# A decoder layer on one core: heads summed on VectorE, layernorm's step on ScalarE, and a re-costed plan

## Chip, cores and metric

The program runs on one core of one Trainium2 chip. The metric is device time in microseconds (us), lower is better. Engines are called by their short names in the profile: PE (TensorE, matrix products), DVE (VectorE), ACT (ScalarE), POOL (GpSimd) and SP (SyncE, which issues the DMAs).

## What is computed

32 sequences of 128 positions with 128 features go through three residual blocks, each followed by a layernorm without gain. All of it is in float32. Cut to its core, for `x` of shape (32, 128, 128):

```python
x = layernorm(x + self_attention(x, W))            # 16 heads of 8 features, no mask
x = layernorm(x + cross_attention(x, ctx, Wq, ...)) # 16 heads, window of 64 positions
x = layernorm(x + ffn(x))                          # two layers, see below

def self_attention(x, W):        # y: x cut into 16 heads of 8
    attn = softmax(y @ y.T / sqrt(8))              # per head, 128 x 128
    o = attn @ x                                   # per head, 128 x 128: the whole x
    return concat_heads(o) @ W                     # W: 16*128 x 128

def layer(x):                    # twice
    q, k, v = shift_token(x) @ wqkv                # 8 heads of 64
    q, k = rotary_xpos(l2norm(q) * qs, l2norm(k) * ks)   # cosines, sines of the swapped halves
    x = x + local_attention(q, k, v) @ wo          # window of 64, softmax
    h = layernorm(shift_token(x)) * lg + lb
    a, g = split(h @ w1 + b1)
    return x + (a * gelu(g)) @ w2 + b2
```

## The kernel before

Everything stays on the chip between the blocks. The 32 sequences are cut into ten groups of 2, 3, 3, 4, 4, 4, 4, 4, 3 and 1 (`SIZES`). There are four stages: self-attention, cross-attention and the two layers. A group passes through the stages one after another, and several groups are in flight at once, each in another stage.

**Order.** No operation is issued where it stands in the code. Each call `op(engine, ns, fn, reads, writes, ...)` records one step with a booked duration in ns. `Plan.issue` (line 132) then simulates the five engines: it keeps a clock per engine, a delay `hop` between engines, a price for a new activation table, a price for a change of TensorE's tile shape, and the free buffers of each ring. Each time it issues the step that can start first. What comes out is a fixed order for each engine's queue, in which the chip then runs, each instruction waiting for its inputs by semaphores. The order in which steps are offered is set by constants at the top: `LAGS` says how far a stage trails the one before it, in units of four sequences; `SPREAD`, `CLOSE` and `EARLY` stretch these places; `AHEAD` bounds how far a step may be drawn forward; among the steps that start within `NEAR` ns, the one recorded first is taken. Steps with `port=True` are those of VectorE and GpSimd that the plan keeps from running beside each other.

**Buffers.** `m` is a ring of eight PSUM banks of 128x512 float32. `big` (128x1032), `mid` (128x520), `xb`, `xc`, `sm` and others are rings in SBUF; `RINGS` and `KEEP` are their sizes and how many are kept back for older steps.

**Self-attention** (`self_half`, line 571) handles one sequence and eight heads: a half. The product with W is moved in front: `zs = x W_h` for each head (TensorE, L579; copied out by ScalarE, L586), with a column of ones behind each head. The scores (L542) are reduced to their maxima (VectorE, L421), GpSimd splits these in two bfloat16 parts (L435, L436), TensorE turns and subtracts them (L442, L452), ScalarE takes exp (L600). Then TensorE multiplies by `zs` in groups of three, three and two heads (L608): the ones' column yields the row sums. VectorE inverts the sums (L617) and multiplies (L618), writing the normalized heads back into `zs`. GpSimd adds the eight heads in a tree, four, two and one wide (L628), and adds the result to the residual tile `x0` (L632).

**Layernorm** (`layernorm`, line 377) runs five times for each group: VectorE takes the statistics (L382, L389), GpSimd makes the factor and the offset with a power (L397 to L400), and VectorE applies both, one 128x128 instruction for each sequence (L407). `feed_forward` then turns the result on TensorE (L373).

**A layer** (`local_batch`, line 790) projects one sequence to q, k and v with three products of 512 columns (L796) that ScalarE copies out (L801). ScalarE squares q and k (L807), VectorE sums the squares (L810), GpSimd raises the sums to -1/2 (L813, L814). GpSimd multiplies the swapped halves by the sines (L824), VectorE multiplies q and k by the cosines (L833), adds both (L837) and scales (L840). TensorE turns q and k (L851, copied by ScalarE at L857), makes the masked scores (L865, L871), VectorE takes maxima (L421), ScalarE the exps with their sums (L466), VectorE divides (L885, L886), TensorE turns (L481, copied out at L488), multiplies by v (L900, L907) and projects (L912, L919). The feed-forward part is L944 to L971. Cross-attention uses the same helpers; its own products are at L649, L663, L689 and L724, its normalization at L750 and L751, and its residual sum at L696.

Of the kernel before, what the change touches and what calls it, by code (L numbers as in the profile page):

```python
# [16 lines left out]
P = 128  # L17
# [11 lines left out]
AHEAD = 430  # L29
LAGS = (0, 1.35, 2.75, 4.1)  # L30
RINGS = (23, 16, 6, 4)
KEEP = (2, 3, 5)
NEAR = 0
EARLY = (0, 0.2)
CLOSE = (0.9, 0.85, 0.9, 1, 1, 1, 1.2, 1.05, 0.85, 0.95)
SPREAD = (1.4, 1.0, 0.7, 1.5)
# [40 lines left out]
class Plan:  # L77

# [51 lines left out]
    def issue(self, ahead, near=80.0, hop=60.0, table_ns=1300.0, tiling_ns=160.0, dma_ns=1800.0):  # L132
# [13 lines left out]
        def time_of(k):  # L146
            e = ops[k][0]
            return max([0.0] + [end[d] + (hop if ops[d][0] != e else 0.0) for d in ops[k][3]])
# [5 lines left out]
        shared = 0.0  # L154
# [5 lines left out]
        while len(order) < n:  # L160
            best = None
            for e in engines:
                choice, least = [], None
                for k, t in ready[e]:
                    if k > first + ahead:
                        continue
                    start = max(clock[e], t, shared if ops[k][7] else 0.0)
# [5 lines left out]
                    for vs in need.values():  # L173
                        q = vs[0].ring
                        if len(q.free) < len(vs) + (0 if q.queue[q.head] in vs else q.keep):
                            ok = False
                            break
                        start = max(start, sorted(q.free)[len(vs) - 1][0] + hop)
# [4 lines left out]
                    if e == "PE" and ops[k][8][0] != state:  # L183
                        start += tiling_ns
# [22 lines left out]
            else:  # L207
                end[k] = clock[e] = s + ns
            if tab:
                table[e] = tab  # L210
            if port:
                shared = end[k]
# [19 lines left out]
def decoder_kernel(ctx: ExitStack, tc: tile.TileContext, a: dict, out: bass.AP):  # L232
# [129 lines left out]
    def turned(src, n):  # L362

        tp, t = Val(mring), Val(mid)
        op("PE", 113 * n, turn(src, tp, n), [src], [tp], hold=[t])
        op("ACT", 140 + 113 * n,
# [10 lines left out]
    def layernorm(src, dst, n):  # L377
# [6 lines left out]
        op("DVE", n * 290, stats, [src], [st])  # L384
# [6 lines left out]
        op("DVE", n * 175, aggr, [st], [mv])  # L391
# [10 lines left out]
        op("POOL", 1100 + 260 * n, rest, [], [mv])  # L402

        def apply():
            x, y = group(src.t), group(dst.t)
            for j in range(n):
                nc.vector.tensor_scalar(  # L407
                    y[:, j, :], x[:, j, :], mv.t[:, 8 + j : 9 + j], mv.t[:, 12 + j : 13 + j],
                    ALU.mult, ALU.add,
                )  # L410

        op("DVE", 200 * n, apply, [mv] + ([src] if src is not dst else []), [dst])
# [4 lines left out]
    def maxima(s, nm):  # L417
        for b in range(2):
            op(
                "DVE", 690,  # L420
# [5 lines left out]
    def minus_max(s):  # L426
# [6 lines left out]
        def parts():  # L433
# [4 lines left out]
        op("POOL", 440, parts, [nm], [hl])  # L438
        mp = Val(mring, lambda t: t[:, 0:64].bitcast(BF16))
        op(  # L440
            "PE", 110,
# [4 lines left out]
        op("ACT", 260, lambda: nc.scalar.copy(mT.t, mp.t), [mp], [mT])  # L446
# [10 lines left out]
    def exps_of(s, sums=None):  # L457
# [4 lines left out]
        for b in range(2):  # L462
# [8 lines left out]
            op("ACT", 4 * (345 if sums else 255) + 60, exps, [s[b], (nm, b)],  # L471
# [3 lines left out]
    def turned_half(e, et, b, eng, src):  # L475
# [9 lines left out]
        op("PE", 4 * 113, pe, [src], [tp], hold=[et])  # L485
        copy = nc.vector.tensor_copy if eng == "DVE" else nc.scalar.copy
        op(eng, 690 if eng == "DVE" else 590,
# [6 lines left out]
    def in_slots(src, n, keep_src, moving):  # L494
# [4 lines left out]
        op("ACT", 140 + 113 * n,  # L499
           lambda: nc.scalar.copy(pv.t[:, 0, every], src.t[:, every]), [src], [(pv, 0)])  # L500
        op("POOL", 316 * n,
# [3 lines left out]
        op("ACT", 140 + 113 * n,  # L505
           lambda: nc.scalar.copy(pv.t[:, 1, every], rest.t[:, every]), [rest], [(pv, 1)])
        op("POOL", 316 * n,
# [26 lines left out]
    def scores_of(s, stationary, moving, hh, window=False):  # L534
# [12 lines left out]
        op("PE", 8 * 62 + 432 * window, pe,  # L547
# [22 lines left out]
    def self_half(j, hh, x0, xT, ys):  # L570
# [3 lines left out]
        for b in range(2):  # L574
# [3 lines left out]
                "PE", 875,  # L578
# [6 lines left out]
                "ACT", 590,  # L585
# [10 lines left out]
        op("PE", 8 * 60, lambda: emit_max(s, mT), [mT, (w_self, 2)], s)  # L596
        e = Val(big, heads)
        for b in range(2):
            op("ACT", 590,
# [3 lines left out]
        for k, (h0, n) in enumerate(((0, 3), (3, 3), (6, 2))):  # L603
# [9 lines left out]
            op("PE", 230 * n, pe, [e] + [(zs, i) for i in range(3)], [oz])  # L613
            rl = Val(small)

            def scale(oz=oz, rl=rl, h0=h0, n=n):
                nc.vector.reciprocal(rl.t[:, 0:n], oz.t[:, 0:n, D])  # L617
                nc.vector.tensor_tensor(  # L618
                    zs.t[:, h0 : h0 + n, 0:D], oz.t[:, 0:n, 0:D],
                    rl.t[:, 0:n].unsqueeze(2).to_broadcast([P, n, D]), ALU.mult,  # L620
                )

            op("DVE", 175 + 30 + 133 * n, scale, [oz], [rl, (zs, ("o", k))])

        z = lambda h0, n: zs.t[:, h0 : h0 + n, 0:D]
        for n, ns in ((4, 1270), (2, 730), (1, 450)):
            op("POOL", ns,
               lambda n=n: nc.gpsimd.tensor_tensor(z(0, n), z(0, n), z(n, n), ALU.add),  # L628
               [], [zs], port=n > 1)
# [493 lines left out]
```

## Time and profile before

| | us |
|---|---|
| median of three runs | 1292.23 |
| lowest and highest | 1289.26, 1293.61 |
| the profiled execution | 1292.12 |
| its span, first to last instruction | 1290.3 |
| mean granted clock of TensorE | 0.987 of full |

The profile's first part gives busy time, share of the span and number of instructions of each engine; PEld are TensorE's weight loads, which overlap its products. Records of TensorE overlap too, because products are pipelined, so groups of it sum to more than the engine's busy time. The chain is the work that ended last, followed back from the end: at each step to what released it. A group has the form "line engine operation out<-in"; `m` stands for any of the eight PSUM banks. For one line, median and extremes of the durations are to be had as well: the power of L813 takes 2895 at least, 2910 in the median and 3996 ns at most.

### The profile page before, as it was taken

What the parts mean: (1) busy time and instruction counts of PE and PEld (TensorE: products, weight loads), DVE (VectorE), ACT (ScalarE), POOL (GpSimd) and SP (SyncE); (2) the same over time, 40 slices, a digit from 0 to 9 for tenths busy, and PEclk for the clock granted to TensorE, in tenths of its full rate; (3) what the DMA queues carried; (4) which work ended last, traced back from release to release, by engine and by line L of the source; (5) the groups of instructions that cost most, each with busy time, mean ns of one, the idle gap of its engine ahead of it and who ended that gap; (6) DMA issues with size and microseconds to landing.
All of it is one profiled execution on the core that took longest, in us unless ns stands there. A gap on an engine that the chain in (4) does not pass through costs nothing.

```text
span 1290.3 us, 27579 instructions
## 1 busy us (share of the span) xinstructions
PE 1213.9 (94%) x9730; PEld 888.0 (69%) x9730; DVE 1070.3 (83%) x2134; ACT 966.2 (75%) x2762; POOL 835.3 (65%) x1094
## 2 busy tenths in 40 slices
PE   7988999999979999999999999999999989999996
PEld 4766677776767865777777667778667657567664
DVE  2677889878968888887798889979899999988786
ACT  4564777777867778777778778858889968879863
POOL 2866657765857389555687468653966963786454
PEclk9999999999989999999999999999999989999999
DMA  9886414240154420732005401330300000000000
GB/s 254 209 213 193 124 39 105 56 128 9 37 136 109 99 56 1 174 89 65 20 25 138 124 1 34 94 95 18 97 2 12 18 18 2 9 1 2 2 1 25
DMA packets 173930, 91.44 MB, mean 71 GB/s; under 512 B 155872, under 2 KB 161888, under 8 KB 173536
## 3 DMA queue, kind: packets, MB, share of 16 engines
q1 hardware_dynamic: 173792, 89.67, 27.5%
q8 instruction: 77, 1.26, 0.4%
q14 instruction: 61, 0.50, 0.1%
HBM read 49.79 MB, written 39.85 MB: 69 GB/s over the span
## 4 chain that ended last, share of the span: by engine, by line
PE 45%; POOL 15%; DVE 14%; ACT 6%; issue 3%; DMA 1%; SPq 0%; POOLq 0%; DVEq 0%; ACTq 0%
PE m L796 6%; POOL sm L813 6%; PE m L481 5%; PE m L944 4%; PE m L608 4%; ACT big L466 3%; PE m L900 3%; PE m L579 3%; PE m L871 3%; PE m L912 3%; POOL big L824 3%; PE m L964 3%; PE m L724 2%; DVE sm L421 2%; PE m L542 2%
## 5 line engine op out<-in xcount | busy, mean ns | idle before, releaser
L466 ACT ACTIVATE big<-m,sm 128x128 f32<-128x128 f32 x1024 | 323.0, 399 | 54.5 <-DVE sm L421 53.9
L421 DVE TENSOR_REDUCE sm<-m 128x4 f32<-128x512 f32 x384 | 245.6, 681 | 45.4 <-PE m L871 21.5
L813 POOL TENSOR_TENSOR sm<-sm,nhalf 128x16 f32<-128x16 f32 x64 | 200.8, 3137 | 36.8 <-DVE sm L810 26.7
L628 POOL TENSOR_TENSOR big<-big 128x512 f32<-128x512 f32 (+2 forms) x192 | 163.2, 850 | 83.8 <-DVE big L618 36.8
L824 POOL TENSOR_TENSOR big<-big,layer_w 128x512 f32<-128x512 f32 x128 | 162.4, 1269 | 76.4 <-ACT big L801 71.1
L796 PE MATMUL m<-layer_w,mid 128*128 128x512 f32 x384 | 193.2, 612 | 4.2 <-DVE xb L971 2.1
L481 PE MATMUL m<-ident,big 128*128 128x128 f32 x1024 | 144.4, 276 | 15.4 <-DVE big L886 9.6
L481 PEld LDWEIGHTS m<-ident,big 128*128 128x128 f32 x1024 | 115.7, 141 | 54.9 <-issue 21.9
L579 PE MATMUL m<-self_w,mid 128*128 128x512 f32 x256 | 131.1, 626 | 7.0 <-DMA self_w<-in_self_w 5.7
L608 PEld LDWEIGHTS m<-big,big 128*128 128x128 f32 x1024 | 123.0, 191 | 13.7 <-issue 7.5
L608 PE MATMUL m<-big,big 128*128 128x129 f32 x1024 | 129.9, 276 | 0.9 <-DVE big L618 0.3
L466 ACT ACTIVATION_READ_ACCUMULATOR big<-m,sm 128x1 f32 x512 | 115.9, 226 | 0.0
L586 ACT COPY big<-m 128x512 f32<-128x512 f32 x128 | 75.1, 600 | 38.8 <-PE m L579 38.0
L618 DVE TENSOR_TENSOR big<-m,sm 128x384 f32<-128x384 f32 (+1 forms) x192 | 98.6, 514 | 6.6
L886 DVE TENSOR_TENSOR big<-big,sm 128x512 f32<-128x512 f32 x128 | 98.2, 767 | 4.6 <-DMA slots<-big 0.2
L542 PEld LDWEIGHTS <-big 72*128 72x128 bf16 x1024 | 72.3, 98 | 41.3 <-issue 20.2
L542 PE MATMUL m<-big,big 72*128 72x128 bf16 x1024 | 87.8, 220 | 9.6 <-DMA big<-slots 8.9
L488 ACT COPY big<-m 128x512 f32<-128x512 f32 x128 | 75.0, 598 | 28.3 <-PE m L481 19.4
L796 PEld LDWEIGHTS m<-layer_w,mid 128*128 128x128 f32 x384 | 64.7, 193 | 42.6 <-issue 27.9
L857 ACT COPY big<-m 128x512 f32<-128x512 f32 x128 | 71.6, 608 | 29.7 <-PE m L851 29.1
L944 PE MATMUL m<-mid,layer_w 128*128 128x512 f32 (+7 forms) x240 | 89.5, 516 | 2.7 <-DVE mid L935 1.5
L488 DVE COPY big<-m 128x512 f32<-128x512 f32 x128 | 82.0, 681 | 11.5 <-PE m L481 10.7
(116 smaller groups left out, 2611.4 us busy)
## 6 DMA issues: line engine op xcount, KB each, us to landing
slots<-big SPq DMA_DIRECT2D x384, 96.0 KB
big<-slots SPq DMA_DIRECT2D x128, 288.0 KB
layer_w<-in_layer_w SPq DMA_DIRECT2D x2, 1877.0 KB
mid<-in_xt SPq DMA_DIRECT2D x5, 256.0 KB
mid<-in_xg SPq DMA_DIRECT2D x5, 256.0 KB
mid<-in_ct SPq DMA_DIRECT2D x5, 256.0 KB
out<-xb SPq DMA_DIRECT2D x5, 256.0 KB
self_w<-in_self_w SPq DMA_DIRECT2D x2, 512.0 KB
```

The lines of the kernel that those rows point to most:

```text
L421: lambda b=b: nc.vector.tensor_reduce(nm.t[:, 4 * b : 4 * b + 4], s[b].t, AX.X, ALU.max, negate=True),
L466: nc.scalar.activation(e.t[:, h, :], s[b].t[:, h - 4 * b, :], AF.Exp, bias=nm.t[:, h : h + 1], accum_out=sums.t[:, h : h + 1] if sums else ...
L481: nc.tensor.transpose(tp.t[:, 128 * c : 128 * c + 128], e.t[:, 4 * b + c, :], ident)
L488: lambda: copy(et.t[:, 4 * b : 4 * b + 4, :], tp.t.rearrange("p (c k) -> p c k", c=4)),
L542: nc.tensor.matmul(s[b].t[:, i, :], st[:, h, :], mv[:, h, :], start=not window and i == 0, stop=i == 3,)
L579: lambda zp=zp, h0=h0: nc.tensor.matmul(zp.t, group(xT.t)[:, j, :], attn_w[:, h0 : h0 + 4, :], start=True, stop=True),
L608: nc.tensor.matmul(oz.t[:, i, :], e.t[:, h0 + i, :], zs.t[:, h0 + i, :], start=True, stop=True,)
L628: lambda n=n: nc.gpsimd.tensor_tensor(z(0, n), z(0, n), z(n, n), ALU.add),
L796: lambda hp=hp, i=i: nc.tensor.matmul(hp.t, group(hT.t)[:, j, :], wqkv[l][:, INNER * i : INNER * (i + 1)], start=True, stop=True),
L813: nc.gpsimd.tensor_tensor(rn.t[:, 0:16], rn.t[:, 0:16], nhalf, ALU.pow)
L824: nc.gpsimd.tensor_tensor(r2.t[:, :, :, d0 : d0 + 32], q[:, :, :, d1 : d1 + 32], tabs[l][:, :, d0 : d0 + 32].unsqueeze(2).to_broadcast([P, ...
L944: lambda t=t, off=off, c0=c0, m=m: nc.tensor.matmul(t.t[:m, every], w1[l][:, off + c0 : off + c0 + m], hT.t[:, every], start=True, stop=True),
```

## The change

1. **Self-attention.** VectorE still inverts the row sums. Then, for each head, one instruction multiplies the head in PSUM by its inverse sum and adds it to the residual tile `x0`, eight for a half. The normalized heads are no longer written to `zs`, and GpSimd's four adds for a half are gone.
2. **Cosines.** The product of q and k with the cosines is made for each of the two projections straight from the PSUM bank, into the tile `qr`, beside ScalarE's copy. It replaces the one product of twice the width that read the copy. `qr` is now taken when the projection is issued.
3. **Layernorm.** The factor and the offset are applied by ScalarE, with one per-partition operand for each, in place of VectorE.
4. **Plan.** All booked durations are new. The delay between engines is now a `TAIL` of the engine that ends and a `HOP` of the one that starts; a follower on the same engine may start at the end of the booking. GpSimd and VectorE's `port` steps now exclude each other by a lock for each side. A change of tile shape is booked at 95 or 150 ns. `AHEAD`, `RINGS`, `KEEP`, `NEAR`, `EARLY`, `CLOSE` and `SPREAD` have new values.

```diff
-AHEAD = 430
+AHEAD = 330
-RINGS = (23, 16, 6, 4)
-KEEP = (2, 3, 5)
-NEAR = 0
-EARLY = (0, 0.2)
+RINGS = (23, 17, 6, 4)
+KEEP = (3, 4, 7)
+NEAR = 60
+EARLY = (0.1, 0.2)
-SPREAD = (1.4, 1.0, 0.7, 1.5)
+SPREAD = (1.3, 1.0, 0.7, 1.5)
...
+    TAIL = {"PE": 165.0, "DVE": 82.0, "ACT": 115.0, "POOL": -75.0, "SP": 0.0}
+    HOP = {"PE": 55.0, "DVE": 32.0, "ACT": 36.0, "POOL": 77.0, "SP": 25.0}
...
-            return max([0.0] + [end[d] + (hop if ops[d][0] != e else 0.0) for d in ops[k][3]])
+            return max([0.0] + [
+                end[d] + (self.HOP[e] if ops[d][0] != e else -self.TAIL[e]) for d in ops[k][3]
+            ])
...
-                    start = max(clock[e], t, shared if ops[k][7] else 0.0)
+                    start = max(clock[e], t)
+                    if e == "POOL" or ops[k][7]:
+                        start = max(start, lock["DVE" if e == "POOL" else "POOL"])
...
-                        start += tiling_ns
+                        start += 95.0 if state == "whole" else 150.0
...
         def apply():
             x, y = group(src.t), group(dst.t)
             for j in range(n):
-                nc.vector.tensor_scalar(
-                    y[:, j, :], x[:, j, :], mv.t[:, 8 + j : 9 + j], mv.t[:, 12 + j : 13 + j],
-                    ALU.mult, ALU.add,
+                nc.scalar.activation(
+                    y[:, j, :], x[:, j, :], AF.Identity,
+                    scale=mv.t[:, 8 + j : 9 + j], bias=mv.t[:, 12 + j : 13 + j],
                 )
-        op("DVE", 200 * n, apply, [mv] + ([src] if src is not dst else []), [dst])
+        op("ACT", 365 * n, apply, [mv] + ([src] if src is not dst else []), [dst])
...
             op(
-                "DVE", 690,
+                "DVE", 598,
                 lambda b=b: nc.vector.tensor_reduce(
...
-            def scale(oz=oz, rl=rl, h0=h0, n=n):
+            def scale(oz=oz, rl=rl, n=n):
+                y = group(x0.t)[:, j, :]
                 nc.vector.reciprocal(rl.t[:, 0:n], oz.t[:, 0:n, D])
-                nc.vector.tensor_tensor(
-                    zs.t[:, h0 : h0 + n, 0:D], oz.t[:, 0:n, 0:D],
-                    rl.t[:, 0:n].unsqueeze(2).to_broadcast([P, n, D]), ALU.mult,
-                )
-            op("DVE", 175 + 30 + 133 * n, scale, [oz], [rl, (zs, ("o", k))])
-        z = lambda h0, n: zs.t[:, h0 : h0 + n, 0:D]
-        for n, ns in ((4, 1270), (2, 730), (1, 450)):
-            op("POOL", ns,
-               lambda n=n: nc.gpsimd.tensor_tensor(z(0, n), z(0, n), z(n, n), ALU.add),
-               [], [zs], port=n > 1)
-        y = lambda: group(x0.t)[:, j, :]
-        op("POOL", 450,
-           lambda: nc.gpsimd.tensor_tensor(y(), y(), z(0, 1)[:, 0, :], ALU.add),
-           [zs], [(x0, j)])
+                for i in range(n):
+                    nc.vector.scalar_tensor_tensor(
+                        y, oz.t[:, i, 0:D], rl.t[:, i : i + 1], y, ALU.mult, ALU.add
+                    )
+            op("DVE", 100 + 205 * n, scale, [oz], [rl, (x0, j)])
...
-               [hT, w_layer[l]], [hp], hold=[qk if i < 2 else vs])
-            op("ACT", 590,
+               [hT, w_layer[l]], [hp], hold=[qk, qr] if i < 2 else [vs])
+            op("ACT", 478,
...
+            if i < 2:
+                op("DVE", 620,
+                   lambda hp=hp, i=i: nc.vector.tensor_tensor(
+                       qr.t[:, i], hp.t.rearrange("p (h d) -> p h d", d=LD),
+                       tabc[l][:, i].unsqueeze(1).to_broadcast([P, LH, LD]), ALU.mult),
+                   [hp, w_layer[l]], [(qr, i)])
...
-        op("POOL", 2600, swap, [qk, w_layer[l]], [r2], port=True)
-        qr = Val(big, four)
-        op("DVE", 1240,
-           lambda: nc.vector.tensor_tensor(
-               qr.t, qk.t.rearrange("p (a h) d -> p a h d", a=2),
-               tabc[l].unsqueeze(2).to_broadcast([P, 2, LH, LD]), ALU.mult),
-           [qk, w_layer[l]], [qr], port=True)
-        op("DVE", 1240, lambda: nc.vector.tensor_tensor(qr.t, qr.t, r2.t, ALU.add), [r2], [qr], port=True)
-        op("POOL", 3200, power, [], [rn])
+        op("POOL", 2237, swap, [qk, w_layer[l]], [r2], port=True)
+        op("DVE", 1140, lambda: nc.vector.tensor_tensor(qr.t, qr.t, r2.t, ALU.add), [r2], [qr], port=True)
+        op("POOL", 3171, power, [], [rn])
```

In the changed file the lines that the prediction names stand some lines lower: the adds of point 1 at L631, the product of point 2 at L811, the step of point 3 at L417.

## The prediction

> **What bounds the kernel now.** I read the page's first part, then the chain that ended last, then the stretches of 100 us, then the groups by form, then short pieces of the timeline. The page and its chain:
>
> ```profile
> span 1290.3 us, 27579 instructions
> PE 1213.9 (94%) x9730; PEld 888.0 (69%) x9730; DVE 1070.3 (83%) x2134; ACT 966.2 (75%) x2762; POOL 835.3 (65%) x1094
> ...
> PE 45%; POOL 15%; DVE 14%; ACT 6%; issue 3%; DMA 1%; SPq 0%; POOLq 0%; DVEq 0%; ACTq 0%
> ```
>
> TensorE is covered for 94%, yet the chain runs over it for only 45%: for the other half somebody makes TensorE's next input just in time, most of all GpSimd and VectorE. TensorE's busy time also holds pipeline ends. Its own need, from its tightest rows in the chain: 760 records of 512 columns (L796, L579, L944) at 0.43 us (L796 x4 in 1.72) are 327 us; 1920 of L608, L912, L964 at 0.112 us (L608 x32 in 3.57), 215; 1728 transposes (L481, L851, L373) at 0.109 us (L481 x12 in 1.31), 188; 3072 of L724, L900, L871 at 0.055 to 0.068 us, some 187; the bf16 scores, masks and rest some 235. Together about 1150 us. So 140 us of the span are waits, refills, start and end. Where they lie:
>
> ```profile
> 0.00:100.00 100.00, 86.80 (x623) 61.61 (x623) 58.26 (x145) 55.67 (x131) 57.93 (x134) 1.00 0.86 225
> ...
> 800.00:900.00 100.00, 98.63 (x875) 76.13 (x874) 86.98 (x197) 76.88 (x233) 57.27 (x83) 1.00 0.28 69
> 900.00:1000.00 100.00, 99.37 (x782) 69.61 (x782) 92.12 (x161) 87.42 (x252) 74.63 (x73) 1.00 0.15 38
> 1000.00:1100.00 100.00, 91.37 (x705) 64.93 (x701) 92.87 (x156) 79.58 (x250) 65.72 (x59) 0.97 0.05 12
> ...
> 1200.00:1290.00 90.00, 77.54 (x589) 55.05 (x587) 67.24 (x161) 54.96 (x175) 43.86 (x58) 0.96 0.03 10
> ```
>
> The columns are PE, PEld, DVE, ACT, POOL, granted clock, DMA share, GB/s. Self-attention's normalization ends at 907 us; behind it, with the two layers alone, VectorE is at 92% and TensorE loses time again behind it.
>
> **The groups the change touches**, by form:
>
> ```profile
> L833 DVE TENSOR_TENSOR big<-big,layer_w 128x1024 f32<-128x1024 f32 x64 | 86.0, 1343 | 3.9 <-ACT big L801 3.8
> ...
> L618 DVE TENSOR_TENSOR big<-m,sm 128x384 f32<-128x384 f32 x128 | 71.5, 558 | 4.4
> L407 DVE TENSOR_SCALAR mid<-mid,sm 128x128 f32<-128x128 f32 x64 | 31.4, 546 | 8.2 <-POOL sm L400 8.2
> ...
> L919 DVE TENSOR_TENSOR xb<-m,xb 128x128 f32<-128x128 f32 x32 | 9.1, 288 | 11.8 <-PE m L912 8.0 <-PE m L740 3.1
> ...
> L954 DVE SCALAR_TENSOR_TENSOR mid<-m,cross_w,mid 128x128 f32<-128x128 f32 x4 | 1.3, 336 | 1.0 <-ACT mid L950 1.0
> ```
>
> Each row gives busy us and the mean ns of one; behind the bar the idle time before it and what ended it. The adds exist today as GpSimd's L628, the sum's nearest kin on VectorE as L954 and L919.
>
> The chain is a path of 1290 us, so I price each part by what it has there: I added up the chain's pieces line by line.
>
> **1. Self-attention's adds leave GpSimd.** L628 (163.2 us) and L632 (31.8) go, 195.0 of GpSimd's 835.3 us. On the chain they have 21.9 + 2.8: **-24.7 us**. What is late next is the same sum, now on VectorE:
>
> **2. The sum on VectorE.** Eight fused multiply-adds of 128x128 per half take the place of three products, 512 in all. Each adds into the same x0 tile, and in the built program each waits for the one before. What such a wait costs:
>
> ```profile
> 592.80 0.18 DVE L617 RECIPROCAL sm<-m 128x3 f32<-128x3 f32 x1 [1.08 <-PE m L608]
> 593.01 0.56 DVE L618 TENSOR_TENSOR big<-m,sm 128x384 f32<-128x384 f32 x1
> ...
> 593.90 0.25 DVE L750 RECIPROCAL sm<-m 128x16 f32<-128x16 f32 x1
> 594.18 0.29 DVE L751 TENSOR_TENSOR mid<-m,sm 128x128 f32<-128x128 f32 x1
> ...
> 598.62 0.56 DVE L618 TENSOR_TENSOR big<-m,sm 128x384 f32<-128x384 f32 x1
> 599.09 0.17 DVE L617 RECIPROCAL sm<-m 128x3 f32<-128x3 f32 x1
> ```
>
> A dependent step starts 30 ns after its forerunner ended (593.90 + 0.25 to 594.18); an independent one 85 ns before that end (598.62 + 0.56 to 599.09). With L954's 336 ns a dependent add takes 0.366 us and the last 0.251: three heads 0.21 + 2 x 0.366 + 0.251 = 1.19 us, two heads 0.81, a half 3.19. Before, from the rows, 0.68 + 0.68 + 0.54 = 1.90. So +1.29 x 64 = **+83 us of VectorE**. On the chain L617 and L618 have 13.2 us; times 3.19/1.90: **+9.0 us**. With L919's 288 ns a half is 2.84; with no price on the wait (0.205 an add) 2.25 and the term +2.4; I take L954, the same operation. Queued behind these adds are maxima and PSUM copies that TensorE waits for.
>
> The Trainium skill, "VectorE: DVE Perf Modes", section "The DRAIN you can't avoid", says that chained operations pay the pipeline's flush with or without a semaphore, so the wait is free. The rows above disagree by 0.115 us a step; by the page's rule a step costs the same either way, and this term would be +2.4 us.
>
> **3. Layernorm's step moves to ScalarE.** L407 is 160 instructions in four forms, 72.3 us, 0.452 each. Unhindered four take 1.10 us (1265.66 in the timeline), but:
>
> ```profile
> 1043.13 4.48 POOL L824 TENSOR_TENSOR big<-big,layer_w 128x512 f32<-128x512 f32 x4
> 1043.21 4.48 DVE L407 TENSOR_SCALAR mid<-mid,sm 128x128 f32<-128x128 f32 x4 [1.64 <-POOL sm L400]
> ...
> 1044.45 0.30 PE L373 MATMUL m<-ident,mid 128*128 128x128 f32 x1 [2.11 <-DVE mid L407]
> ```
>
> Each instruction waits out one of GpSimd's, and TensorE's transpose of the tile waits with it. On the chain L407 has 34.2 us, 76 instructions' worth. ScalarE's nearest row is L466 of the same size with one operand per partition: 12 in 3.21 us without the accumulator, 0.27 each; with the accumulator read 0.35. The new form has two such operands; I take 0.31: 76 x 0.31 = 23.6, so **-10.6 us** (-13.7 to -7.6). ScalarE gets 160 x 0.31 = 50 us and stays under 82%; queued behind are its evictions. Table loads in the built order fall from 36 to 34 (2.6 us). If ScalarE is late there, TensorE's turn of the normalized tile is late too.
>
> The Trainium skill, "ScalarE: Activation LUTs", section "What ACT_TABLE_LOAD costs", speaks against this: every per-partition operand adds about 93 ns. With 0.27 + 0.09 = 0.36, an estimate, the term would be -6.8 us; no row here has two such operands.
>
> **4. The cosines' product.** 64 of L833 (86.0 us) become 128 of 512 columns straight from PSUM, nearest L971's form at 685 ns, 0.60 in a run as L488 (four in 2.47): 78 us. On the chain L833 has 10.0 us; the product now stands beside ScalarE's copy, but its successor L837 still needs GpSimd's L824, so I book half, **-5 us** (0 to -10). A bank of PSUM is held until VectorE has read it too.
>
> **5. Port.** L407 and L833 no longer collide with GpSimd. GpSimd's power (L813) takes 2910 ns in the median and 3137 in the mean, 14.5 us in all; 36% lies on the chain. **-2 us**.
>
> **6. GpSimd's queue.** 165 us of GpSimd stay on the chain (L813 72.1, L824 33.5). Load falls by 23%, so these start sooner where they queued behind an add. Bounds 0 and 23% of 165 = 38; starts, not durations, shrink: I take a tenth, **-16 us**.
>
> **7. Order.** Every booking is rewritten, so every queue is re-ordered; TensorE's work is the same 8547 instructions, SyncE's DMA issues the same 560. TensorE changes its tile shape 278 times against 239; sixteen scores took 1.32 against 1.16 us, so 39 x 0.16 = 6 at most: **+3 us**. The rest of the re-planning I book at nothing, between -35 (half the idle and refill time of the middle) and +80: a half's adds are booked at 1.94 us, and by part 2 take 3.19, so 64 x 1.25 = 80 us of VectorE stand in no booking.
>
> Sum: -24.7 + 9.0 - 10.6 - 5 - 2 - 16 + 3 = **-46.3 us**. The profiled execution took 1292.1 us for its span of 1290.3; that gives a span of 1244 and **1246 us**, against the median of 1292.2 alike. VectorE's total hardly changes (+83 - 72 - 8 - some 5 of lock), but it moves from the crowded last 400 us into the first 900.
>
> **Rivals.**
> - *Order pays more.* With the idle time of the first and last 100 us as it is (13 and 12 us) over the need of 1150, and -35 from re-planning: 1211 us. For it: bookings now match rows (L421 598 for 0.60 in a run, L824 2237 for 2 x 1105). Against it: the adds' do not. 14%.
> - *The gain is eaten by banks and buffers.* PSUM has eight banks; held longer for adds and cosines they stall projections. Giving back 30 us: 1276 (1268 to 1296). For it: ScalarE's waits for PE are spread over all evictions, so TensorE runs few banks ahead. 16%, 6 of them within 0.3% of before.
> - *Slower: VectorE becomes the bound in the first 900 us.* If all 80 unbooked us of the adds fall on TensorE, 1246 + 80 = 1326; it ends above 1296 once more than 50 of 80 land. Against it: from 100 to 900 us VectorE is idle 16%, 2 us in the 14 that a half takes, more than 1.25. 12%.
>
> **Numbers.** Forecast 1246, its own range 1225 to 1268, 58%. The range 1208 to 1296 leaves out the slow rival and the best part of the fast one, some 18%. Faster by over 0.3%, about what this measurement can tell: 58 + 14 + 10 = 82%; within 6%; slower 12%.
>
> **What would show it.** Right: GpSimd near 640 us, VectorE near 1070, ScalarE near 1015; adds of some 336 ns starting 0.36 apart; ScalarE's steps 0.27 to 0.36 apart; VectorE above 85% before 900 us and below 90% after; the chain over GpSimd below 12%. Wrong: adds 0.2 apart (part 2 was dear), TensorE waiting for L631 or for banks read at L811 (rivals two and three), or a chain still on GpSimd's power.

## The result and the profile after

The changed kernel takes **1338.69 us** in the median of four runs (1336.35 to 1339.71) against 1292.58 (1289.26 to 1293.61) for the kernel before on the same chip: a ratio of 1.0359, with a 95% interval of 1.0335 to 1.0382. It is 46 us slower; 46 us faster was forecast. The page of the profiled execution, its first lines and the chain by engine:

```profile
span 1334.5 us, 27571 instructions
...
PE 1222.3 (92%) x9675; PEld 883.0 (66%) x9730; DVE 1077.5 (81%) x2358; ACT 1017.5 (76%) x2920; POOL 623.1 (47%) x838
...
PE 43%; DVE 30%; ACT 15%; issue 5%; POOL 3%; DMA 2%; SPq 1%; DVEq 0%; POOLq 0%; ACTq 0%
DVE mid L631 8%; ACT big L476 7%; DVE sm L431 6%; PE m L800 5%; PE m L589 5%; PE m L491 5%; PE m L947 4%; PE m L618 3%; PE m L903 3%; PE m L915 3%; DVE big L843 2%; PE m L874 2%; DVE big L889 2%; PE m L726 2%; PE m L967 2%
```

GpSimd lost 212 us of work and nearly left the chain (15% to 3%), VectorE gained 7 us in all, and the chain now runs over VectorE for 30% instead of 14%. The adds alone (L631) hold 8% of it, some 105 us. The two chains are not of one length: that of before could be followed back only to 214 us after the start, so its shares add up to 84% of the span; that of the changed kernel reaches the start. The clock is no cause: it is granted at 0.994 here and at 0.987 before. The groups by form of the changed kernel that answer to those shown of before (busy us, mean ns of one, idle time before them):

```profile
L631 DVE SCALAR_TENSOR_TENSOR mid<-m,sm,mid 128x128 f32<-128x128 f32 x512 | 179.7, 351 | 18.2
...
L811 DVE TENSOR_TENSOR big<-m,layer_w 128x512 f32<-128x512 f32 x128 | 85.5, 683 | 18.6 <-PE m L800 14.2
L805 ACT COPY big<-m 128x512 f32<-128x512 f32 x128 | 77.3, 632 | 26.3 <-DVE big L811 13.1
...
L417 ACT ACTIVATE mid<-mid,sm 128x128 f32<-128x128 f32 x64 | 27.2, 512 | 11.8 <-POOL sm L410 11.8
```

An add takes 351 ns (336 assumed). ScalarE's layernorm step (L417) takes 512 ns in the mean of its commonest form, and a new wait stands ahead of ScalarE's copy L805: for VectorE's product L811, which reads the same bank of PSUM. In the built program 57 of these 128 copies wait for VectorE's product, and 60 of the 128 products wait for the copy. The two readers of a bank stand one after the other, where I had written "beside" in the prediction. The stretches of 100 us, with columns as before:

```profile
0.00:100.00 100.00, 82.54 (x591) 58.35 (x594) 64.67 (x191) 55.80 (x128) 25.82 (x86) 1.00 0.81 212
...
800.00:900.00 100.00, 92.94 (x715) 65.73 (x718) 81.08 (x181) 77.53 (x221) 51.81 (x66) 1.00 0.28 69
900.00:1000.00 100.00, 90.08 (x751) 65.98 (x756) 82.13 (x174) 77.96 (x229) 44.91 (x56) 1.00 0.16 40
1000.00:1100.00 100.00, 95.92 (x774) 69.16 (x776) 88.41 (x153) 87.88 (x269) 66.09 (x62) 1.00 0.05 13
```

TensorE, at 99% from 800 to 1000 us before, is at 90 to 93%, and neither VectorE nor GpSimd is busier than it was there. One number places the loss. Self-attention's last normalization started at 906.5 us of 1290.3, so 383.8 us lay behind it. In the changed kernel the last adds start at 952.9 us:

```profile
L631 DVE SCALAR_TENSOR_TENSOR mid<-m,sm,mid x512: 350/351/353, 30.2 to 952.9; 128x128 f32<-128x128 f32 x171
```

These are least, median and greatest ns, then the first and last start. Behind it lie 381.6 us. **The whole loss lies ahead of the end of self-attention**, where the adds are. One half of them in the timeline:

```profile
611.57 0.18 DVE L629 RECIPROCAL sm<-m 128x3 f32<-128x3 f32 x1 [1.55 <-ACT big L498]
611.79 1.12 DVE L631 SCALAR_TENSOR_TENSOR mid<-m,sm,mid 128x128 f32<-128x128 f32 x3
612.83 0.17 DVE L629 RECIPROCAL sm<-m 128x3 f32<-128x3 f32 x1
613.03 1.12 DVE L631 SCALAR_TENSOR_TENSOR mid<-m,sm,mid 128x128 f32<-128x128 f32 x3
614.08 0.16 DVE L629 RECIPROCAL sm<-m 128x2 f32<-128x2 f32 x1
614.27 0.74 DVE L631 SCALAR_TENSOR_TENSOR mid<-m,sm,mid 128x128 f32<-128x128 f32 x2
614.93 0.68 DVE L431 TENSOR_REDUCE sm<-m 128x4 f32<-128x512 f32 x1
```

From 611.57 to 614.93 are 3.36 us (3.19 forecast, 1.90 before): 64 x 1.46 = 93 us more of VectorE's queue, an estimate from this one half. A maximum (L431) that TensorE and ScalarE need stands right behind it. The waits of the changed kernel (engine and line, what it waited for: us in total, times, longest):

```profile
POOL big L833 <- ACT big L805: 166.9, 32, 21.0
POOL pad L445 <- DVE sm L431: 145.6, 41, 19.0
...
ACT big L476 <- DVE sm L431: 87.3, 59, 5.0
```

The same three rows were 71.1, 70.0 and 53.9 us before. GpSimd now waits some 170 us longer in the first two: most of the work taken from it has turned into waiting. ScalarE's exps wait 33 us longer for VectorE's maxima. TensorE waits for the adds themselves, here three of the rows that name them:

```profile
PE m L452 <- DVE mid L631: 3.3, 4, 1.6
...
PE m L589 <- DVE mid L631: 2.5, 6, 1.0
...
PE m L552 <- DVE mid L631: 1.9, 5, 0.6
```

All such rows add up to 13.6 us of TensorE's products and 15.3 us of its weight loads; the products that the adds replace (L618) had 3.8 and 6.4 us before. All of the products' waits that VectorE ended rose from 33.4 to 65.0 us.

### The profile page after: what moved, and what is told of

It reads as the page before. It is cut to its first block, busy times and chain, and to the rows that moved or that the text cites. A ratio compares the mean times of both kernels' runs of the same rounds, so it can differ in the third digit from the quotient of the medians.

```text
span 1334.5 us, 27571 instructions
## 1 busy us (share of the span) xinstructions
PE 1222.3 (92%) x9675; PEld 883.0 (66%) x9730; DVE 1077.5 (81%) x2358; ACT 1017.5 (76%) x2920; POOL 623.1 (47%) x838
## 4 chain that ended last, share of the span: by engine, by line
PE 43%; DVE 30%; ACT 15%; issue 5%; POOL 3%; DMA 2%; SPq 1%; DVEq 0%; POOLq 0%; ACTq 0%
DVE mid L631 8%; ACT big L476 7%; DVE sm L431 6%; PE m L800 5%; PE m L589 5%; PE m L491 5%; PE m L947 4%; PE m L618 3%; PE m L903 3%; PE m L915 3%; DVE big L843 2%; PE m L874 2%; DVE big L889 2%; PE m L726 2%; PE m L967 2%
## 5 line engine op out<-in xcount | busy, mean ns | idle before, releaser
L476 ACT ACTIVATE big<-m,sm 128x128 f32<-128x128 f32 x1024 | 325.0, 400 | 88.3 <-DVE sm L431 87.3
L431 DVE TENSOR_REDUCE sm<-m 128x4 f32<-128x512 f32 x384 | 245.7, 682 | 39.3 <-PE m L874 27.1
L833 POOL TENSOR_TENSOR big<-big,layer_w 128x512 f32<-128x512 f32 x128 | 153.1, 1196 | 185.6 <-ACT big L805 166.9
L823 POOL TENSOR_TENSOR sm<-sm,nhalf 128x16 f32<-128x16 f32 x64 | 208.3, 3255 | 41.7 <-DVE sm L820 40.1
L631 DVE SCALAR_TENSOR_TENSOR mid<-m,sm,mid 128x128 f32<-128x128 f32 x512 | 179.7, 351 | 18.2
L491 PE MATMUL m<-ident,big 128*128 128x128 f32 x1024 | 147.5, 278 | 35.6 <-DVE big L889 26.7
L589 PE MATMUL m<-self_w,mid 128*128 128x512 f32 x256 | 128.8, 611 | 9.5 <-DMA self_w<-in_self_w 5.5
L618 PE MATMUL m<-big,big 128*128 128x129 f32 x1024 | 131.6, 279 | 2.6 <-DVE mid L631 0.8
L618 PEld LDWEIGHTS m<-big,big 128*128 128x128 f32 x1024 | 122.9, 192 | 14.1 <-issue 5.5
L476 ACT ACTIVATION_READ_ACCUMULATOR big<-m,sm 128x1 f32 x512 | 118.8, 233 | 0.0
L811 DVE TENSOR_TENSOR big<-m,layer_w 128x512 f32<-128x512 f32 x128 | 85.5, 683 | 18.6 <-PE m L800 14.2
L805 ACT COPY big<-m 128x512 f32<-128x512 f32 x128 | 77.3, 632 | 26.3 <-DVE big L811 13.1
L596 ACT COPY big<-m 128x512 f32<-128x512 f32 x128 | 75.1, 620 | 28.2 <-PE m L589 27.6
L552 PEld LDWEIGHTS <-big 72*128 72x128 bf16 x1024 | 72.2, 97 | 36.6 <-issue 18.7
L843 DVE TENSOR_TENSOR big<-big,sm 128x1024 f32<-128x1024 f32 x64 | 87.1, 1361 | 11.0 <-POOL sm L824 10.2
L552 PE MATMUL m<-big,big 72*128 72x128 bf16 x1024 | 88.4, 219 | 5.6 <-DVE mid L631 1.9
L498 ACT COPY big<-m 128x512 f32<-128x512 f32 x128 | 78.6, 633 | 12.6 <-PE m L491 10.8
```

The costliest lines, as they stand in the source:

```text
L431: lambda b=b: nc.vector.tensor_reduce(nm.t[:, 4 * b : 4 * b + 4], s[b].t, AX.X, ALU.max, negate=True),
L476: nc.scalar.activation(e.t[:, h, :], s[b].t[:, h - 4 * b, :], AF.Exp, bias=nm.t[:, h : h + 1], accum_out=sums.t[:, h : h + 1] if sums else ...
L491: nc.tensor.transpose(tp.t[:, 128 * c : 128 * c + 128], e.t[:, 4 * b + c, :], ident)
L498: lambda: copy(et.t[:, 4 * b : 4 * b + 4, :], tp.t.rearrange("p (c k) -> p c k", c=4)),
L552: nc.tensor.matmul(s[b].t[:, i, :], st[:, h, :], mv[:, h, :], start=not window and i == 0, stop=i == 3,)
L589: lambda zp=zp, h0=h0: nc.tensor.matmul(zp.t, group(xT.t)[:, j, :], attn_w[:, h0 : h0 + 4, :], start=True, stop=True),
```

## Experiments

Theory A: the adds lengthen VectorE's in-order queue and cost the path about half of what they add, while GpSimd's relief was never on the path. Theory B: the new plan's order is bad. Theory C: the layernorm step on ScalarE, or the cosines read from PSUM, do the harm. Times are medians; a ratio is to the kernel before on the same chip in the same runs, with its 95% interval.

### One part undone and planned anew

`e1_no_adds` has the sum as before (three products, GpSimd's adds), `e2_no_cos` the cosines' product as before, `e3_no_ln` the layernorm step as before; the rest is the changed kernel. `e4_booked` only books the adds longer:

```diff
-            op("DVE", 100 + 205 * n, scale, [oz], [rl, (x0, j)])
+            op("DVE", 30 + 410 * n, scale, [oz], [rl, (x0, j)])
```

> The changed kernel with the old sum alone: VectorE's products into zs, GpSimd's tree of adds. Theory A (the adds cost VectorE 3.37 us a half where the plan books 1.94, 92 us of the run in no booking, and VectorE is late for the maxima and divisions that TensorE needs): most of the 46 us come back, 1270 to 1295 us. Theory C (the cosines' product and ScalarE's copy read one bank in turn): little comes back, 1325 to 1345. Theory P (the new bookings and constants make a worse order whatever the operations): 1320 to 1350.

> The changed kernel with the old cosines' product alone, twice as wide from the copy in SBUF. Theory A: 1330 to 1350 us, VectorE gets 64 wide products with GpSimd's port in place of 128 from PSUM. Theory C (57 of ScalarE's 128 copies of q and k wait for VectorE's read of the same bank in the built program, and 60 of VectorE's reads wait for the copy): 1300 to 1320. Theory P: 1330 to 1350.

> The changed kernel with layernorm's step back on VectorE. Theory A: VectorE gets 50 to 72 us more, 1340 to 1365 us. A theory that ScalarE's step, 490 ns where VectorE took 340 unhindered, is what costs: 1310 to 1325. Theory P: 1330 to 1350.

> The changed kernel with the same operations, but the adds booked as the chip runs them: 30 + 410 n ns, 1.26 and 0.85 us for three and two heads, in place of 100 + 205 n. Theory A in its strict form (the missing booking is what costs): 1290 to 1315 us. Theory A in its wide form (the VectorE time itself costs, booked or not): 1325 to 1345. Theory P: 1325 to 1350, since all the other bookings stay.

Measured: e1 1323.88 us (1.0257 [1.0224, 1.0290]), e2 1361.26 (1.0537 [1.0504, 1.0571]), e3 1346.23 (1.0422 [1.0384, 1.0461]), e4 1319.14 (1.0218 [1.0185, 1.0252]). Against the changed kernel's 1338.69 that is -15, +23, +8 and -20 us. Theory A's forecast for e1 failed (the time lies in theory P's range), and e2 and e4 lie in none of the ranges. But each of these plans anew, so the order of every queue differs too. What an order is worth by itself had to be known first.

### The order by itself

`e5_plan_only` has before's operations under the changed plan; `e6_old_plan` the new operations under before's plan, with the adds booked at 205 + 290n; three controls change one constant of the plan and no operation:

```diff
-NEAR = 0      (before)
+NEAR = 20     (c1_before_near), 40 (c3_before_near40)
-NEAR = 60     (after)
+NEAR = 40     (c2_after_near)
```

> The kernel before in its operations, with the changed plan alone: new bookings, delays, lock and constants (the old operations booked by their rows: 260 + 140 n for L618, 1140 for the product of 1024, 275 for a layernorm step with the lock, GpSimd's adds 1280, 680, 430, 430). Theory P (the new plan is the loss; the operations gain): 1335 to 1365 us. Theory A (the adds are the loss): 1275 to 1300.

> The changed kernel's operations with the plan of before: its delays, lock, constants and bookings, the three new operations booked in its manner (205 + 290 n for the adds, 690 for a cosines' product, 400 for a layernorm step). Theory P: the gain that the operations hold shows, 1250 to 1285 us. Theory A: the adds cost under this plan too, 1300 to 1330. Theory O (any other order than the one tuned costs some per cent): 1300 to 1330 as well, and then the two controls beside it are slow too.

> Control: the kernel before with NEAR 20 in place of 0, the same operations, bookings and delays in a slightly other order. Theory O (the order of before is a lucky one that its constants were fitted to): 1305 to 1330 us. The others: 1288 to 1300.

> Control: the changed kernel with NEAR 40 in place of 60. Theory O: anywhere from 1320 to 1360 us, more than 8 us from 1339. The others: 1332 to 1346.

> Second control: the kernel before with NEAR 40. Theory O (its order is a fitted one, and most others of the same plan lose 2 to 3%): 1310 to 1335 us. If c1 was an accident: 1288 to 1300.

Measured: e5 1321.40 (1.0227 [1.0199, 1.0254]), e6 1348.30 (1.0447 [1.0402, 1.0492]), c1 1326.44 (1.0269 [1.0236, 1.0302]), c2 1353.09 (1.0463 [1.0428, 1.0497]), c3 1342.45 (1.0400 [1.0369, 1.0431]). The very operations of before, in another order of the same planner, lose 35 and 52 us (c1 and c3); e5, e6 and c3 lie outside every range stated for them. So the kernel before is at a good order among its neighbours, and a re-planned kernel does not price a part to better than some 15 to 50 us. Three readings follow. e1 to e4 settle nothing by themselves. The 29 us of e5 do not show the new plan worse than any other order (B is neither shown nor refuted by it). And under before's plan, too, the new operations are no faster than before.

### Before's own order, one part swapped in

Here the plan is computed with before's bookings and dependences, so that every step keeps its place; only what a step issues is changed. In `f1_fixed_adds` VectorE's step issues the eight fused adds, and GpSimd's four steps issue nothing:

```diff
-                nc.vector.tensor_tensor(
-                    zs.t[:, h0 : h0 + n, 0:D], oz.t[:, 0:n, 0:D],
-                    rl.t[:, 0:n].unsqueeze(2).to_broadcast([P, n, D]), ALU.mult,
-                )
+                for i in range(n):
+                    nc.vector.scalar_tensor_tensor(
+                        y, oz.t[:, i, 0:D], rl.t[:, i : i + 1], y, ALU.mult, ALU.add
+                    )
...
-            op("POOL", ns,
-               lambda n=n: nc.gpsimd.tensor_tensor(z(0, n), z(0, n), z(n, n), ALU.add),
-               [], [zs], port=n > 1)
+            op("POOL", ns, lambda: None, [], [zs], port=n > 1)
```

In `f2_fixed_ln` the layernorm step is issued on ScalarE, at places that the plan chose for VectorE; `f4_fixed_adds_ln` has both.

> The kernel before with its own plan, bookings and order, in which the adds alone are swapped: VectorE's three products of a half become eight fused adds into the residual tile in the same places of its queue, and GpSimd's four adds issue nothing. Every other queue is instruction by instruction that of before. Theory A (the adds' 94 us of VectorE cost time by themselves): 1310 to 1345 us. Theory O (the loss is the loss of a fitted order): 1270 to 1300, since this order is kept. If the recorded forecast's reasoning on the operations holds: 1265 to 1280.

> The kernel before with its own order, in which only layernorm's step is issued on ScalarE, at the place in the order at which VectorE had it. The recorded forecast gives this part 10.6 us (7 to 14): 1275 to 1287 us. A theory that ScalarE's 490 ns in front of its evictions costs more than VectorE gains: 1293 to 1305.

> Both of these swaps together, in the order of before. If the two parts add up: f1 plus f2 less 1292. Theory A: 1300 to 1335 us. Theory O: 1260 to 1290, faster than before.

Measured: f1 **1339.79** (1.0379 [1.0364, 1.0395]), f2 1298.99 (1.0061 [1.0044, 1.0079]), f4 1331.97 (1.0312 [1.0295, 1.0329]). The adds alone, in an order that has nothing of the new plan, lose 49 us, as much as the whole change. The page and the waits of f1:

```profile
PE 1232.2 (92%) x9685; PEld 892.6 (67%) x9730; DVE 1138.5 (85%) x2454; ACT 966.5 (72%) x2762; POOL 647.0 (48%) x838
```

```profile
POOL pad L435 <- DVE sm L421: 185.7, 44, 23.7
POOL big L818 <- ACT big L795: 109.9, 24, 14.0
ACT big L466 <- DVE sm L421: 70.0, 48, 5.7
```

GpSimd's busy time fell by 188 us and its first two waits grew by 155. What the relief is worth by itself is not shown: no run takes the adds from GpSimd without putting them on VectorE. TensorE's rows that name the adds (L620 here) come to 24.8 us, and 39.8 of its weight loads; the products' waits that VectorE ended rose from 33.4 to 61.5 us, much as in the changed kernel. The last adds start at 954.8 us of a span of 1338.0, 383.2 before its end, just as in the changed kernel. The layernorm step costs 8 us by itself in this order and gives 8 us back once the adds are in (f4 against f1): its sign depends on what else is in the queues.

### The changed kernel's own order, the adds made lighter

`g1_light_adds` issues one add for each group instead of two or three, 192 of 512, so that five of eight heads are missing from the sum. `g2_no_wait` issues all 512, but each writes to a slice of the residual tile beside the one that it reads, so none waits for the one before it; the sum over the heads is left out.

```diff
-                for i in range(n):
+                for i in range(1):              (g1)
...
-                        y, oz.t[:, i, 0:D], rl.t[:, i : i + 1], y, ALU.mult, ALU.add
+                        group(x0.t)[:, (j + 1 + i) % G, :], oz.t[:, i, 0:D], ...   (g2)
```

> The changed kernel in its own order, of which each instruction of the adds but the first of a group is left out (192 of 512 are issued, five of eight heads are missing from the sum): 320 x 0.38 = 120 us less of VectorE at the places where the adds stand. Theory A: 1265 to 1300 us. Theory P or O: 1315 to 1335, since the order is the loss.

> The changed kernel in its own order with as many adds, of which each writes beside the slice that the next one reads (the heads' sum is left out: every add takes the unsummed residual), so that no add waits for the one before it. By the rows each of the 512 gets 0.10 to 0.115 us shorter in VectorE's queue, 50 to 59 us in all. If time falls here as it fell in g1 (65 us for 120), 1306 to 1315 us: the wait is half of what the adds cost. If the wait is free, 1335 to 1341.

Measured: g1 **1274.17** (0.987 [0.985, 0.989]) and g2 **1300.59** (1.0084 [1.0061, 1.0107]): 65 and 38 us below the changed kernel. In g1 some 320 x 0.375 = 120 us of VectorE's queue are gone, and 0.54 of each came off the time; in f1 93 were added (GpSimd relieved with it) and 0.52 of each went onto it. Two kernels with different orders, moved in opposite directions, agree on the mean of some 100 us. The page of g1:

```profile
PE 1204.5 (95%) x9675; PEld 885.7 (70%) x9730; DVE 976.0 (77%) x2038; ACT 1015.6 (80%) x2920; POOL 623.2 (49%) x838
...
PE 67%; ACT 12%; DVE 10%; DMA 4%; issue 2%; POOL 2%; SPq 1%; DVEq 0%; POOLq 0%; ACTq 0%
```

and its waits, of which one row is enough:

```profile
ACT big L476 <- DVE sm L431: 46.1, 46, 2.4
```

The chain runs over TensorE for 67% and over VectorE for 10%, and ScalarE's wait for the maxima fell from 87.3 to 46.1 us. The same half without the chain of waits, in g2's timeline:

```profile
619.99 0.87 DVE L631 SCALAR_TENSOR_TENSOR mid<-m,sm,mid 128x128 f32<-128x128 f32 x3
620.88 0.18 DVE L629 RECIPROCAL sm<-m 128x3 f32<-128x3 f32 x1
621.09 0.87 DVE L631 SCALAR_TENSOR_TENSOR mid<-m,sm,mid 128x128 f32<-128x128 f32 x3
621.88 0.16 DVE L629 RECIPROCAL sm<-m 128x2 f32<-128x2 f32 x1
622.07 0.61 DVE L631 SCALAR_TENSOR_TENSOR mid<-m,sm,mid 128x128 f32<-128x128 f32 x2
```

Three adds take 0.87 us instead of 1.12, two 0.61 instead of 0.74: 0.63 us a half, 40 us in all, of which 38 came off the time. In this order the waits between the adds are worth most of the loss. The range stated for g2 carried g1's rate over and began 5 us too high: nearly all of the first 40 us come off, and the 80 us more that g1 takes away bring only 26 more. So the half is a mean over a large step and no fixed rate. The products' waits that VectorE ended fall along with the time, from 65.0 us to 42.4 in g2 and 30.7 in g1.

### The changed kernel's own order, the other parts undone

`g3_kept_no_cos`: the 128 products from PSUM issue nothing, and the wide product of before is issued right ahead of the sum with the sines. `g4_kept_no_ln`: the layernorm step is issued on VectorE at ScalarE's places.

```diff
-                   lambda hp=hp, i=i: nc.vector.tensor_tensor(qr.t[:, i], ...   (g3)
+                   lambda: None,
...
-                nc.scalar.activation(                                            (g4)
+                nc.vector.tensor_scalar(
```

> The changed kernel in its own order, in which the two products of the cosines from PSUM issue nothing and the one wide product from the copy stands just ahead of the sum with the sines. No bank has two readers in turn any more. Theory C: 1315 to 1330 us. The recorded forecast (the part gains 5 us, up to 10): 1340 to 1350. In e2, where the plan was free to re-order, it took 1361.

> The changed kernel in its own order with layernorm's step issued on VectorE at the places where ScalarE has it. The recorded forecast (the part gains 7 to 14 us): 1345 to 1355. As in f1 to f4 (the step gains 8 where VectorE carries the adds): 1345 to 1350. If ScalarE's step is the dearer one: 1325 to 1337.

Measured: g3 1378.30 (1.0702 [1.0653, 1.0752]) and g4 1361.24 (1.0553 [1.0528, 1.0579]). Undoing either costs, 40 and 23 us, more than any range stated: **C finds no support.** In this order both parts are better kept. The 40 are not the worth of the cosines' part: the wide products of g3 hold VectorE for 84.7 us against 85.5, so what changed is mainly their place, late and in one piece of 1.3 us, and that place is my choice. In g4, too, VectorE's steps stand where the plan had put ScalarE's. The cosines' part in before's order was not run.

### Versions meant to be faster

`h1_two_sums` is the changed kernel with two accumulators: odd heads go into a second tile, which GpSimd adds once for each sequence. `h2_cos_only` has the cosines' part alone. Both book VectorE's and ScalarE's steps longer (by a tenth and by 6%), and have constants of the plan chosen anew.

```diff
+                z = odd[turn_of.setdefault((id(x0), j), len(turn_of)) % len(odd)]
...
+                    o = z if (h0 + i) % 2 else y
...
-            op("DVE", 100 + 205 * n, scale, [oz], [rl, (x0, j)])
+            op("DVE", 210 + 277 * n, scale, [oz], [rl, (x0, j)])
```

> The changed kernel with the sum taken in two: even heads are added into the residual tile, odd heads into a second tile, so that an add waits only for the last but one, and GpSimd joins both once a sequence. The adds are booked at 210 + 277 n, all of VectorE's and ScalarE's bookings are raised by a tenth and TensorE's by a fiftieth for slack, and AHEAD, NEAR, KEEP and CLOSE are chosen anew for that. From g2 (1300.6 in the old order, without the join) less what true bookings gave in e4 (20): 1270 to 1295 us. If the fitted order of before is the whole matter: 1310 to 1330.

> The cosines' product from PSUM alone, the part that gained 39 us in a kept order (g3): the sum is GpSimd's, layernorm's step VectorE's as before; the changed plan with VectorE and ScalarE booked 6% higher and constants chosen anew. If that gain holds and the order is as good as an average one (e5 with 1321): 1275 to 1300 us. If any order that was not fitted on the chip loses: 1310 to 1330.

Measured: h1 1310.71 (1.0142 [1.0113, 1.0171]), h2 1310.99 (1.0151 [1.0125, 1.0177]). Neither beats the kernel before; both lie in the range stated for the case that any order not fitted on the chip loses. Two accumulators do remove the waits, as h1's timeline shows:

```profile
480.67 0.35 DVE L639 SCALAR_TENSOR_TENSOR mid<-m,sm,mid 128x128 f32<-128x128 f32 x1
480.93 0.34 DVE L639 SCALAR_TENSOR_TENSOR odd<-m,sm,zero 128x128 f32<-128x128 f32 x1
481.19 0.34 DVE L639 SCALAR_TENSOR_TENSOR mid<-m,sm,mid 128x128 f32<-128x128 f32 x1
481.45 0.17 DVE L636 RECIPROCAL sm<-m 128x3 f32<-128x3 f32 x1
```

The adds start 0.26 us apart. h1 is 28 us below the changed kernel, but its order and bookings differ too, so how much of the 28 is due to the accumulators is not shown.

## Why the prediction was wrong

Its sums of busy time were nearly right: GpSimd 623 us (640 forecast), VectorE 1077.5 (1070), ScalarE 1017.5 (1015). The time was off by 93 us because of how those loads were turned into time.

**Part 2, the sum on VectorE, is the step that failed**: "On the chain L617 and L618 have 13.2 us; times 3.19/1.90: +9.0 us". Measured in the kept order (f1): +49, with what GpSimd's relief gave already in it. The size of the work was nearly right (3.36 us a half for 3.19, because an add takes 351 ns). The price of it was not: in the changed kernel the adds alone have some 105 us of the chain, where the forecast left L617 and L618 together 22. A chain's share tells which microseconds ended last in one execution. It does not tell what happens when 1.46 us more stand in front of the maxima and divisions that follow a half in the same in-order queue. About half of the added time reached the end, in the mean (f1, g1), and nearly all of the part that is waiting between the adds (g2). The part named the risk itself ("Queued behind these adds are maxima and PSUM copies that TensorE waits for") and put no price on it.

The premise "The chain is a path of 1290 us" was wrong as well. The chain of before starts at 214 us, and 22 of the 64 halves run ahead of that, so a third of them had no price at all. This alone does not explain the miss: scaled to all 64 the term would be +14, an estimate from the same rows.

The rule weighed there, in the Trainium skill, "VectorE: DVE Perf Modes", section "The DRAIN you can't avoid", measured on copies there, is that a semaphore between chained operations "costs nothing extra". It does not hold for these adds: taking only the waits away (g2) moved their starts from 0.39 to 0.27 us apart and the time by 38 us. I had taken the rows' side, rightly; the +2.4 us given for the rule, though, rests on L919's 288 ns, and with the 336 that I took it would be +5.1.

**Part 1 (-24.7) and part 6 (-16)** gave nothing that shows, and no run prices them apart from part 2. GpSimd's work and its share of the chain went as forecast, but most of the same microseconds came back as waits for VectorE's maxima and ScalarE's copies. My reading is that what was "late next" was not a row with a fixed length but the producer that GpSimd had been running just behind.

**Part 3 (-10.6)**: +8 alone (f2), -8 beside the adds (f4 against f1), -23 in the new order (g4). The steps are dearer than the 0.31 us that I took: four in 1.71 us, the shortest single one 478 ns.

```profile
987.51 1.71 ACT L417 ACTIVATE xc<-xb,sm 128x128 f32<-128x128 f32 x4
```

That is 0.41 apart, above the range given (0.27 to 0.36). The Trainium skill's rule, "ScalarE: Activation LUTs", section "What ACT_TABLE_LOAD costs", with two per-partition operands gives 186 + 2 x 93 + 0.833 x 128 = 479 ns for one, an estimate that the 478 bears out.

**Part 4 (-5, 0 to -10)**: not shown. Undoing it in the new order costs 40 (g3), which holds the price of a place too, and the version with this part alone (h2), in an order of its own, did not gain. That the two readers of a bank would wait for each other was missed; those waits are 13.1 us on ScalarE and 3.5 on VectorE.

**Part 5 (-2)** was not tried by itself. The shorter power steps that it booked are not there: in the changed kernel GpSimd's power (L823) takes 3255 ns in the mean and 208.3 us in all, where L813 had 3137 and 200.8.

**Part 7, order (+3, and 0 within -35 to +80)**: the range was wide for good reason. Orders of the same operations differ by 35 and 52 us. That the rest would be worth about nothing was a guess: all three other orders of before's operations that ran (c1, c3, e5) are slower, by 29 to 52 us.

**The rivals.** The third, "VectorE becomes the bound in the first 900 us", named the right place, and the adds the right cause. That its price of 1326 came within 13 us is luck: it charged the whole 80 unbooked microseconds (91 by the trace) where about half reached the end, and added them to a sum that held 40 us of gains on GpSimd that do not show. It was given 12% for one argument: that VectorE is idle for 16% there, "2 us in the 14 that a half takes, more than 1.25". This failed. As I read it, the idle time lies between waits, and an in-order queue can't save it up for a long step. VectorE did not even become busier (82% from 100 to 900 us, 83.8% before; above 85% was what I wanted to see): the stretch grew instead. So VectorE is not simply full; that the place in the queue is what costs is argued from the waits, since no run moves the adds to other places of the same queue and changes nothing else. The second, banks held longer, has rows too: besides those 13.1 and 3.5 us, TensorE waits for the adds, as forecast for this sign (13.6 us and 15.3 of its weight loads), at products such as L589 and L552. By the code these read nothing that the adds write, but need a bank. Whether a bank is late because it is held longer or because the adds start late is not told apart. The first, a better order, did not come.

What stays open: the parts do not add up. f4 is at +41 with the adds and the layernorm step, and the whole change at +46, so cosines and new order together cost some 5 here, while undoing the cosines costs 40 in g3. How much of the 46 the new order costs can't be told, since no run has all the new operations in before's order. Whether two accumulators in a well-fitted order would beat the kernel before is open too.

## What to carry to other kernels

Price work that is added to a loaded in-order queue by swapping it into the kept order, one part for each run; in this case its share of the present chain was no price, and the engine's idle share no cover. See first how far back the chain reaches. Work taken from an engine that already waits can come back as waiting. A chain of sums into one tile paid the wait at every step (0.39 us from start to start, against 0.27), and two accumulators removed it. Where a planner rewrites the order, run the old operations in a neighbouring order first: if that alone moves the time by as much as the effect, re-planned variants tell nothing about a part.

## What the runs showed that was not expected

- The fused add of 128x128 takes 351 ns when it waits for the one before and 343 when it doesn't (medians of L631 in the changed kernel and in g2); its kin L954 took 336.
- One constant of the plan (`NEAR`) moves the same operations from 1291.9 to 1326.4 us (c1) and from 1290.1 to 1342.5 (c3).
- The mean granted clock of the profiled executions, 0.974 to 0.994, does not follow the time: 0.987 before, 0.994 for the changed kernel, 0.975 for c1.
- Where only the adds differ within a kept order, and between the two kernels, what lies behind the start of the last self-attention step on VectorE hardly moves, over spans from 1274 to 1338 us: 383.8 us before, 381.6 after, 383.2 in f1, 380.1 in g1, 380.8 in g2. In other orders it does: 394.1 in h1, and some 399 in c1 and 413 in c3.
